# Inverse roots of the norms: a power on GpSimd in place of a square root on ScalarE and a reciprocal on VectorE

## The chip, the cores and the metric

The kernel runs on one core of one Trainium2 chip. The metric is the device time of one execution in microseconds (us); lower is better. One core has five engines with instruction queues of their own: TensorE (PE in the profile; PEld is its weight load), VectorE (DVE), ScalarE (ACT), GpSimd (POOL) and SyncE (SP), which here only issues DMAs. Each queue runs in its own order and waits by semaphores for what other engines produce.

## The reference

The network has 16 stages in a row on an x of 4 batches x 512 tokens x 128 features, float32. Each stage is an attention, a feed-forward or a state-space block on a layer norm of x, added to x:

```python
def _layernorm(x, axis=-1, eps=1e-05):
    m = jnp.mean(x, axis=axis, keepdims=True)
    v = jnp.var(x, axis=axis, keepdims=True)
    return (x - m) / jnp.sqrt(v + eps)

x = x + _L0_attn_a_ref(_layernorm(x, axis=-1), ...)
x = x + _L0_ffn_ref(_layernorm(x, axis=-1), ...)
...
x = x + _L3_ffn_ref(_layernorm(x, axis=-1), ...)
```

Two stages have inverse roots of their own. L1a scales each token of its output by `lax.rsqrt(mean(square(y)) + 1e-6)`. L1b norms its input a second time, `x * lax.rsqrt(mean(x * x) + EPS) * w`, and its output as well, with EPS = 1.1920929e-07.

## The kernel before

x stays in SBUF as 16 tiles of 128 tokens x 128 features, four to a batch; batches are called b0 to b3. The stages run in the order L0a, L0f, L0b, L0f, L1a, L1f, L1b, L1f, L2a, L2f, L2b, L2f, L3a, L3f, L3b, L3f: "a" and "b" are the two mixers of a layer, "f" its feed-forward block.

The layer norm is spread over three engines. When a batch of x has been updated (x<-x,ps in line 443, one VectorE instruction of 128x512), `moments` takes mean and variance of its four tiles on VectorE (bn_stats, bn_aggr: ln_st and ln_mv in the profile). `roots` then turns the variances of one to three batches into inverse roots (ln_rs): one square root on ScalarE with eps as its bias (line 385), and one reciprocal on VectorE (line 389). A root of three batches has 12 columns, that of one batch 4. `centred` writes xn = (x - mean) * root, one VectorE instruction for each of the four tiles of a batch (line 393). `transposed` turns xn on TensorE into PSUM (ps_tr, line 351) and copies it on ScalarE to xT (line 365), from which the stage's matmuls (all in line 346) read. After xn of a batch, GpSimd adds the output bias to x in some stages (x<-x,rows, line 438).

Near the end of a stage the norm of b0 to b2 is made for the next one (`normed_ahead`), while b3 is still computed; b3's own root, four columns, follows at the start of the next stage or within it.

A table of ScalarE functions must be active before its functions run. Square root, exp, silu, sigmoid and tanh need several, and the compiler puts a load (ACT_TABLE_LOAD, booked on the line of the instruction that needs it) wherever the next function isn't in the active one. `prime` (line 410) is an activation on one column whose only effect is to have the table loaded at that place.

The order of each engine's queue is made by a scheduler when the program is built, from its own estimates, except that instructions given to `keep_in_program_order` keep the order of the source among each other on their engine. The square root in `roots` is given to it always; the reciprocal and the centring only where the caller passes `keep`. TensorE's matmuls are nearly all given to it.

In L1a, `output` takes the mean of squares of a batch on TensorE (ps_m), the root of it in line 1353 and 1368 (rs, 4 columns), and adds the product to x (line 1371). In L1b, `roots` (lines 1500 to 1505) takes two roots of the same variances, one with 1 + EPS and EPS * 1e-5 folded in, side by side in a tile rs of 2 x 16 columns, and `finish` takes 8 columns (two batches) through `rsqrt` (line 355). What else comes up below: the memsets of L0b's v (line 809) and nm (816), L0f's sm_m and sm_e (softmax of the router, 472 to 474) and sg (740), L2b's and L3b's wc (2014), da (2343) and hc (2362, 2367), L1a's mask and th (1152, 1120), and L3f's rz (2627, at the end of L3a) and h (2790).

Of the kernel before, what the change touches and what calls it, by code (L numbers as in the profile page):

```python
# [11 lines left out]
F32 = mybir.dt.float32  # L12
AF = mybir.ActivationFunctionType
ALU = mybir.AluOpType
# [4 lines left out]
P = 128  # L19
B, S, D = 4, 512, 128  # L20
# [12 lines left out]
class Pack:  # L33
# [3 lines left out]
    def __init__(self):  # L37
        self.groups = {}
        self.at = {}
        self.rows = {"rows": [], "late": []}  # L40
        self.row_at = {}
# [233 lines left out]
class Net:  # L275
    def __init__(self, ctx, tc, pk, dram):
        self.ctx, self.tc, self.nc, self.pk = ctx, tc, tc.nc, pk
        nc = self.nc
        cp = ctx.enter_context(tc.tile_pool(name="const", bufs=1))
        self.cp = cp  # L280
        self.x = cp.tile([P, NC, D], F32, name="x")

        self.st = cp.tile([P, NC, 6], F32, name="ln_st")
        self.mv = cp.tile([P, NC, 2], F32, name="ln_mv")
        self.rs = cp.tile([P, NC], F32, name="ln_rs")
        self.xn = cp.tile([P, NC, D], F32, name="xn")
        self.xT = cp.tile([P, NT], F32, name="xT")
        self.final = self.ahead = False
        self.extra = ()

        x_in = dram["x"].rearrange("b (j p) d -> p (b j) d", p=P)
        for b in range(B):
            nc.sync.dma_start(self.x[:, CB * b : CB * b + CB], x_in[:, CB * b : CB * b + CB])
        self.w, self.dram = {}, dram
        self.second, self.first, self.zeroth = ExitStack(), ExitStack(), ExitStack()
        self.l1a, self.m0 = ExitStack(), ExitStack()
        second = self.second.enter_context(tc.tile_pool(name="second", bufs=1, side="right"))
        first = self.first.enter_context(tc.tile_pool(name="first", bufs=1, side="right"))
        zeroth = self.zeroth.enter_context(tc.tile_pool(name="zeroth", bufs=1, side="right"))
        self.load(cp, "const")  # L300
        self.load(zeroth, *FIRST[:1])
        self.rows = {}
        self.load_rows(cp, "rows")
        self.load(first, *FIRST[1:])
        self.load(second, *SECOND)

        self.ident = cp.tile([P, P], F32, name="ident")
        make_identity(nc, self.ident)
        self.ones = cp.tile([P, P], F32, name="ones")
        nc.gpsimd.memset(self.ones, 1.0)  # L310
        self.eps = {}
        for n, v in (("1e-5", 1e-5), ("1e-6", 1e-6), ("f32", 1.1920929e-07)):
            self.eps[n] = cp.tile([P, 1], F32, name="eps" + n.replace("-", "_"))
            nc.gpsimd.memset(self.eps[n], v)
        self.primed = cp.tile([P, 1], F32, name="primed")

    def load(self, pool, *groups):
# [34 lines left out]
        if pin:  # L352
            self.tc.keep_in_program_order(i)

    def rsqrt(self, out, in_, eps, scale=1.0):

        self.nc.scalar.activation(out, in_, AF.Sqrt, bias=self.eps[eps], scale=scale)
        self.nc.vector.reciprocal(out, out)

    def transposed(self, pp, tag, outT, tok, pin=False):  # L360

# [20 lines left out]

    def roots(self, b0, b1, keep=lambda i: i):
        cs = slice(CB * b0, CB * b1)
        i = self.nc.scalar.activation(
            self.rs[:, cs], self.mv[:, cs, 1], AF.Sqrt, bias=self.eps["1e-5"]
        )
        self.tc.keep_in_program_order(i)
        keep(self.nc.vector.reciprocal(self.rs[:, cs], self.rs[:, cs]))

    def centred(self, b, keep=lambda i: i):
        for c in range(CB * b, CB * b + CB):
# [14 lines left out]

    def prime(self, fn):

        i = self.nc.scalar.activation(self.primed, self.eps["1e-5"], fn)  # L410
        self.tc.keep_in_program_order(i)

    def norm(self, pp, first=B - 1):
# [761 lines left out]
    def L1a(self):  # L1175
# [3 lines left out]
        nc, tc = self.nc, self.tc  # L1179
        with ExitStack() as es:  # L1180
# [3 lines left out]
            keep = tc.keep_in_program_order  # L1184
# [154 lines left out]
            def output(b):  # L1339
                pm = pp.tile([P, CB], F32, tag="mm", name="ps_m")  # L1340
                for j in range(CB):
                    for g in range(2):
                        self.mm(
                            pm[:, j : j + 1],
                            sq[b][:, g, j * P : j * P + P],
                            self.ones[:, 0:1],
                            start=g == 0,
                            stop=g == 1,
                            pin=True,
                        )  # L1350
                rs = rp.tile([P, CB], F32, name="rs")
                keep(
                    nc.scalar.activation(
                        rs, pm, AF.Sqrt, bias=self.eps["1e-6"], scale=1.0 / D
                    )
                )
                px = pp.tile([P, CB, D], F32, tag="mm", name="ps_x")
                for j in range(CB):
                    for g in range(2):
                        self.mm(  # L1360
                            px[:, j],
                            gt[b][:, g, j * P : j * P + P],
                            self.W("a1_ow")[:, g * P : g * P + P],
                            start=g == 0,
                            stop=g == 1,
                            pin=True,
                        )
                nc.vector.reciprocal(rs, rs)
                xb = self.x[:, CB * b : CB * b + CB]
                for j in range(CB):  # L1370
                    nc.vector.scalar_tensor_tensor(
                        xb[:, j], px[:, j], rs[:, j : j + 1], xb[:, j], ALU.mult, ALU.add
                    )
                self.moments(b)
# [11 lines left out]
            for b in range(B):  # L1386
                self.bias_x(b, "a1_ob")
                keys(b)
                within(b, 0)
                if b + 1 < B:  # L1390
                    features(b + 1, "k", 0)
                else:
                    self.prime(AF.Sqrt)
                    output(0)
                products(b)
                others(b)
                if b == 0:
                    self.normed(B - 1, B)
                    self.prime(AF.Silu)
                if b + 1 < B:  # L1400
                    features(b + 1, "k", 1)
                else:
                    output(1)
                within(b, 1)
                if b + 1 < B:
                    for g in range(2):
                        features(b + 1, "q", g)
                    values(b + 1)
                    gate(b + 1)
                else:  # L1410
                    output(2)
                if b == 0:
                    turned(B - 1)
                if b < 2:
                    self.ternary(f"w{b + 1}", pp.tile([P, 1], F32, tag="mm", name="ps_w"))
                sums(b)
# [58 lines left out]
    def L1b(self):  # L1475
# [4 lines left out]
        nc, tc = self.nc, self.tc  # L1480
        SC, EPS, LAG = 32.0**-0.5, 1.1920929e-07, 3
        with (
# [9 lines left out]

            mv = self.mv
            rs = sp.tile([P, 2, NC], F32, name="rs")
            tiny = sp.tile([P, 1], F32, name="tiny")
            nc.gpsimd.memset(tiny, EPS * 1e-5)
            x0 = sp.tile([P, NC, D], F32, name="x0")
            xh, xT = self.xn, self.xT

            def roots(b0, b1):  # L1500
                cs = slice(CB * b0, CB * b1)
                var = mv[:, cs, 1]
                nc.scalar.activation(rs[:, 0, cs], var, AF.Sqrt, bias=tiny, scale=1.0 + EPS)
                nc.scalar.activation(rs[:, 1, cs], var, AF.Sqrt, bias=self.eps["1e-5"])
                nc.vector.reciprocal(rs[:, :, cs], rs[:, :, cs])


            def centred(out, b, k, eng):
# [31 lines left out]
            q, k, v, ema, a, aT, cT, mixed, y, t = ({} for _ in range(10))  # L1540
# [98 lines left out]
            def finish(b0):  # L1639

                m2 = ms[:, CB * b0 : CB * b0 + 2 * CB]
                self.rsqrt(m2, m2, "f32", scale=1.0 / D)
                for b in (b0, b0 + 1):
                    for j in range(CB):
                        c = CB * b + j
# [807 lines left out]
    def L3a(self):  # L2453
# [3 lines left out]
        nc, tc = self.nc, self.tc  # L2457
        H = S // 2
        with ExitStack() as es:
            sp = es.enter_context(tc.tile_pool(name="l3a_s", bufs=1))  # L2460
            pp = es.enter_context(tc.tile_pool(name="l3a_p", bufs=2, space=PSUM))
            keep = tc.keep_in_program_order
# [4 lines left out]
                out=tri,  # L2467
                in_=tri,
# [42 lines left out]
            bias = self.W("a3_b")  # L2511
            one = self.ones[:, 0:1].to_broadcast([P, S])
            f, ex, v, km, em, wt, kc, r, rz, pv, po, ps = ({} for _ in range(12))
# [166 lines left out]
            for b in range(B):  # L2680
# [35 lines left out]
                masked(b, 3)  # L2716
                if b == 0:
                    self.normed(B - 1, B)
                    self.prime(AF.Exp)
                if b + 1 < B:  # L2720
                    values(b + 1)
                    for i in range(4):
# [21 lines left out]
    def L3f(self):  # L2744

        nc, tc = self.nc, self.tc
        keep = tc.keep_in_program_order
        with (
# [61 lines left out]
            self.mamba_turn(2, bank)  # L2810
            inputs(1)
            self.normed(B - 1, B)
            self.prime(AF.Sigmoid)
            states(1)
            inputs(2)
            self.mamba_turn(3, bank)
# [103 lines left out]
```

## Time and profile before

| | |
|---|---|
| median of 3 runs | 2416.75 us (2408.03 to 2416.97) |
| the profiled execution | 2416.53 us, its span 2414.5 us |
| granted TensorE clock, mean | 0.931 of full |
| square roots on ScalarE in line 385 | 31, about 0.30 us each |
| reciprocals in line 389 | 31, 0.17 to 0.23 us |
| table loads on ScalarE, all lines | 109, 1.283 us each |
| centring on VectorE, line 393 | 240, median 0.342 us |

A row of the profile's timeline reads: start in us, length in us, engine, line, operation, the tile written and the tiles read, partitions x elements, and how many alike were joined. In square brackets stands how long the engine had been idle before it, and what it waited for. The answer for one line lists its instructions with the shortest, median and longest duration in ns, and then who sat waiting for them, how long and how many times.

### The profile page before, as it was taken

The numbers are of one execution on the slowest core, as the hardware profiler recorded it, in microseconds if no ns is written. First come the engines' busy times: TensorE is split into PE (matmuls) and PEld (weight loads), VectorE is DVE, ScalarE is ACT, GpSimd is POOL, SyncE is SP. The second block draws the span as 40 slices with busy tenths as digits, with TensorE's granted clock in tenths as the row PEclk, the third lists the DMA queues.
The fourth block names the chain that finished last, engine by engine and source line by source line (L and its number), as shares of the span: only waits on it lengthen the run. The fifth ranks groups of instructions, "written<-read, shape, count | busy, mean of one in ns | idle before, by whom it ended". The sixth has DMA issues, their size and how long they took to land.

```text
span 2414.5 us, 33686 instructions
## 1 busy us (share of the span) xinstructions
PE 2154.8 (89%) x12151; PEld 1017.6 (42%) x12151; DVE 1731.8 (72%) x3413; ACT 1287.0 (53%) x2550; POOL 610.7 (25%) x443
## 2 busy tenths in 40 slices
PE   7999999999899998999877789888869998888868
PEld 2343334643333334667444446542214666422213
DVE  6666666589998775656464674678997657678995
ACT  4555555279845665342442453666655445466643
POOL 1100010010000001022162410038872014248871
PEclk9999999999899998998866989998989999998989
DMA  3000001400000000410200025334542520044540
GB/s 144 1 1 1 1 1 43 100 1 2 2 1 2 1 1 18 109 18 13 97 1 1 0 46 91 67 122 139 159 146 51 95 49 2 1 121 141 161 152 18
DMA packets 68886, 127.85 MB, mean 53 GB/s; under 512 B 9329, under 2 KB 29297, under 8 KB 68081
## 3 DMA queue, kind: packets, MB, share of 16 engines
q1 hardware_dynamic: 68720, 125.71, 19.6%
q8 instruction: 96, 1.57, 0.3%
q14 instruction: 70, 0.57, 0.1%
HBM read 119.91 MB, written 5.64 MB: 52 GB/s over the span
## 4 chain that ended last, share of the span: by engine, by line
PE 65%; DVE 16%; issue 8%; ACT 6%; DMA 2%; POOL 1%; SPq 1%; POOLq 0%; DVEq 0%; ACTq 0%
PE ps_o L346 14%; PE ps_s L346 9%; PE ps_st L346 6%; PE ps_c L346 5%; PE ps L346 4%; PE ps_g L346 4%; DVE hc L2362 3%; PE ps_x L346 3%; PE ps_u L346 2%; PE ps_v L346 2%; PE ps_qk L346 2%; PE ps_du L346 2%; DVE ps_du L2357 2%; PE ps_tr L351 2%; DVE e L839 2%
## 5 line engine op out<-in xcount | busy, mean ns | idle before, releaser
L2367 POOL TENSOR_TENSOR hc<-hc,cr 128x1024 f32<-128x1024 f32 x126 | 297.4, 2361 | 113.8 <-DVE hc L2362 107.9
L2362 DVE TENSOR_TENSOR_SCAN hc<-da,ps_du 128x1024 f32<-128x1024 f32 x128 | 291.1, 2276 | 0.0
L346 PE MATMUL ps_s<-k,q 32*128 32x512 f32 (+3 forms) x1088 | 256.6, 601 | 10.8 <-DVE mx L839 8.6
L538 ACT ACTIVATE e<-ps_s,mx 128x512 f32<-128x512 f32 x256 | 172.6, 686 | 139.4 <-DVE mx L533 132.8
L346 PE MATMUL ps_du<-du,spread 64*128 64x512 f32 x512 | 162.1, 705 | 66.0 <-DVE hc L2362 65.7
L2343 ACT ACTIVATE da<-da,am 128x512 f32<-128x512 f32 x248 | 166.3, 716 | 63.7 <-DMA da<-dram 48.8
L346 PE MATMUL ps<-xT,w_L2f 128*128 128x512 f32 (+1 forms) x416 | 193.1, 611 | 0.0
L925 DVE TENSOR_REDUCE nm<-ps_s 128x1 f32<-128x512 f32 x256 | 162.7, 684 | 37.5 <-PE ps_s L346 27.8
L1011 ACT ACTIVATE e<-ps_st 128x512 f32<-128x512 f32 x256 | 138.4, 595 | 88.7 <-PE ps_s L346 61.1
L533 DVE TENSOR_REDUCE mx<-ps_s 128x2 f32<-128x1024 f32 x128 | 150.9, 1219 | 43.8 <-PE ps_s L346 43.6
L2357 DVE TENSOR_TENSOR ps_du<-ps_du,br 128x1024 f32<-128x1024 f32 x128 | 155.0, 1211 | 26.9 <-PE ps_du L346 26.9
L850 ACT ACTIVATE e<-e,mx 128x512 f32<-128x512 f32 (+3 forms) x256 | 140.3, 550 | 21.9 <-DVE mx L839 21.3
L346 PE MATMUL ps_st<-q,k 32*128 32x512 f32 x512 | 143.7, 645 | 0.0
L346 PE MATMUL ps_s<-q,k 64*128 64x512 f32 x512 | 129.1, 618 | 2.2 <-ACT e L538 1.7
L346 PE MATMUL ps_c<-e,vz 128*64 128x512 f32 x512 | 123.5, 604 | 0.8 <-POOL vz L549 0.8
L1934 DVE SCALAR_TENSOR_TENSOR t<-ps,w_L2f,t 128x512 f32<-128x512 f32 (+1 forms) x104 | 76.7, 747 | 61.6 <-PE ps L346 39.7
L346 PEld LDWEIGHTS ps_s<-k,q 32*128 32x128 f32 x1088 | 89.0, 192 | 75.0 <-DVE mx L839 50.2
L346 PEld LDWEIGHTS ps_du<-du,spread 64*128 64x128 f32 x512 | 45.9, 203 | 175.0 <-issue 115.0
L839 DVE CUSTOM_DVE_ANT_0 e<-ps_s,tri 128x512 f32<-128x512 f32 (+3 forms) x256 | 109.6, 485 | 8.8 <-PE ps_s L346 8.8
L346 PEld LDWEIGHTS ps<-xT,w_L2f 128*128 128x128 f32 (+1 forms) x416 | 75.5, 190 | 95.8 <-issue 75.5
L549 POOL TENSOR_TENSOR vz<-v,z 128x512 f32<-128x512 f32 x32 | 33.4, 1044 | 321.9 <-DVE z L547 292.9
L659 DVE TENSOR_TENSOR hc<-hc,wt 128x1024 f32<-128x1024 f32 x80 | 94.7, 1188 | 23.1 <-ACT hc L1937 12.2
(499 smaller groups left out, 4199.8 us busy)
## 6 DMA issues: line engine op xcount, KB each, us to landing
da<-dram SPq DMA_DIRECT2D x124, 256.0 KB
da<-dram SPq DMA_DIRECT2D x124, 255.5 KB
wt<-dram SPq DMA_DIRECT2D x144, 128.0 KB
wt<-dram SPq DMA_DIRECT2D x32, 256.0 KB
dram<-dl SPq DMA_DIRECT2D x16, 256.0 KB
wt<-dram SPq DMA_DIRECT2D x16, 224.0 KB
wt<-dram SPq DMA_DIRECT2D x16, 192.0 KB
wt<-dram SPq DMA_DIRECT2D x16, 160.0 KB
```

The source lines that it names most:

```text
L346: i = self.nc.tensor.matmul(out, lhsT, rhs, start=start, stop=stop)
L533: nc.vector.tensor_reduce(mx, sc, AX.X, ALU.max, negate=True)
L538: nc.scalar.activation(es[n][:, hh], sc[:, hh], AF.Exp, bias=mx[:, hh : hh + 1], accum_out=z[m][:, j, hh : hh + 1],)
L659: nc.vector.tensor_tensor(h, h, wt[b, k][:, r:e], ALU.mult)
L839: red = nc.vector.tensor_tensor_reduce(e[:, i, :w], sc[i][:, :w], tri[:, S - w :], -1.0, BIG, ALU.add, ALU.min, mx[:, i : i + 1],)
L850: nc.scalar.activation(e[:, i, :w], e[:, i, :w], AF.Exp, bias=mx[:, i : i + 1], scale=-1.0, accum_out=z[:, i : i + 1],)
L925: nc.vector.tensor_reduce(nm[:, j, i, 9:10], sc, AX.X, ALU.max, negate=True)
L1011: keep(nc.scalar.activation(es_[n][:, i], sc, AF.Exp))
L2343: nc.scalar.activation(da[n][:, t, t:], src[:, t:], AF.Exp, scale=am[:, at : at + 1])
L2357: keep(nc.vector.tensor_tensor(dx[n], dx[n], br, ALU.mult))
L2362: keep(nc.vector.tensor_tensor_scan(h, a, x, 0.0, ALU.mult, ALU.add))
L2367: keep(nc.gpsimd.tensor_tensor(hc[n], hc[n], cr, ALU.mult))
```

## The change

The inverse root is no longer a square root on ScalarE and a reciprocal on VectorE. `roots` adds eps to the variance on GpSimd and raises the sum there to the power -0.5, against a column of -0.5 broadcast over the operand. `rsqrt`, and the roots of L1b, do the scaling and the adding on VectorE and the power on GpSimd. None of these instructions is pinned unless the caller passes `keep`; the square root was. Four primes go: those for the square root and back to silu in L1a, that for exp in L3a after b0, and the second for sigmoid in L3f. Of the columns of constants, the three eps and L1b's tiny go, `some` and `half` come.

```diff
-    def rsqrt(self, out, in_, eps, scale=1.0):
-        self.nc.scalar.activation(out, in_, AF.Sqrt, bias=self.eps[eps], scale=scale)
-        self.nc.vector.reciprocal(out, out)
+    def rsqrt(self, out, in_, eps, scale, keep=lambda i: i):
+        keep(self.nc.vector.tensor_scalar(out, in_, scale, eps, ALU.mult, ALU.add))
+        self.inverse(out, keep)
+
+    def inverse(self, a, keep=lambda i: i):
+        half = self.half.to_broadcast(list(a.shape))
+        keep(self.nc.gpsimd.tensor_tensor(a, a, half, ALU.pow))
...
     def roots(self, b0, b1, keep=lambda i: i):
         cs = slice(CB * b0, CB * b1)
-        i = self.nc.scalar.activation(
-            self.rs[:, cs], self.mv[:, cs, 1], AF.Sqrt, bias=self.eps["1e-5"]
-        )
-        self.tc.keep_in_program_order(i)
-        keep(self.nc.vector.reciprocal(self.rs[:, cs], self.rs[:, cs]))
+        keep(self.nc.gpsimd.tensor_scalar(self.rs[:, cs], self.mv[:, cs, 1], 1e-5, None, ALU.add))
+        self.inverse(self.rs[:, cs], keep)
...
                 rs = rp.tile([P, CB], F32, name="rs")
-                keep(
-                    nc.scalar.activation(
-                        rs, pm, AF.Sqrt, bias=self.eps["1e-6"], scale=1.0 / D
-                    )
-                )
+                self.rsqrt(rs, pm, 1e-6, 1.0 / D)
...
-                nc.vector.reciprocal(rs, rs)
                 xb = self.x[:, CB * b : CB * b + CB]
...
                 else:
-                    self.prime(AF.Sqrt)
                     output(0)
                 products(b)
                 others(b)
                 if b == 0:
                     self.normed(B - 1, B)
-                    self.prime(AF.Silu)
...
             def roots(b0, b1):
                 cs = slice(CB * b0, CB * b1)
                 var = mv[:, cs, 1]
-                nc.scalar.activation(rs[:, 0, cs], var, AF.Sqrt, bias=tiny, scale=1.0 + EPS)
-                nc.scalar.activation(rs[:, 1, cs], var, AF.Sqrt, bias=self.eps["1e-5"])
-                nc.vector.reciprocal(rs[:, :, cs], rs[:, :, cs])
+                nc.vector.tensor_scalar(
+                    rs[:, 0, cs], var, 1.0 + EPS, EPS * 1e-5, ALU.mult, ALU.add
+                )
+                nc.vector.tensor_scalar(rs[:, 1, cs], var, 1e-5, None, ALU.add)
+                self.inverse(rs[:, :, cs])
...
-                self.rsqrt(m2, m2, "f32", scale=1.0 / D)
+                self.rsqrt(m2, m2, EPS, 1.0 / D)
...
                 if b == 0:
                     self.normed(B - 1, B)
-                    self.prime(AF.Exp)
...
             self.normed(B - 1, B)
-            self.prime(AF.Sigmoid)
             states(1)
```

More of the change, by code (lines that the diff above doesn't have):

```diff
@@ L310, in __init__ @@
         nc.gpsimd.memset(self.ones, 1.0)
[L311 to L314, printed above, removed]
+        self.some = cp.tile([P, 1], F32, name="some")
+        nc.gpsimd.memset(self.some, 1e-5)
+        self.half = cp.tile([P, 1], F32, name="half")
+        nc.gpsimd.memset(self.half, -0.5)
         self.primed = cp.tile([P, 1], F32, name="primed")
@@ L408, in prime @@
     def prime(self, fn):
-        i = self.nc.scalar.activation(self.primed, self.eps["1e-5"], fn)
+        i = self.nc.scalar.activation(self.primed, self.some, fn)
         self.tc.keep_in_program_order(i)
@@ L1494, in L1b @@
             rs = sp.tile([P, 2, NC], F32, name="rs")
-            tiny = sp.tile([P, 1], F32, name="tiny")
-            nc.gpsimd.memset(tiny, EPS * 1e-5)
             x0 = sp.tile([P, NC, D], F32, name="x0")
```

## The prediction, made before the changed kernel ran

> **What bounds the kernel now.** I read the page first: busy time by engine, then the chain that ended last.
>
> ```profile
> PE 2154.8 (89%) x12151; PEld 1017.6 (42%) x12151; DVE 1731.8 (72%) x3413; ACT 1287.0 (53%) x2550; POOL 610.7 (25%) x443
> PE 65%; DVE 16%; issue 8%; ACT 6%; DMA 2%; POOL 1%; SPq 1%; POOLq 0%; DVEq 0%; ACTq 0%
> ```
>
> TensorE sets the end, but a third of the chain lies elsewhere, at the seams between stages, where TensorE waits for a normed x. The answer for the line that takes the square root shows what the change can touch.
>
> ```profile
> L385 ACT ACTIVATE ln_rs<-ln_mv,eps1e x31: 296/300/319, 8.9 to 2386.7; 128x4 f32<-128x4 f32 x16, 128x12 f32<-128x12 f32 x14, 128x8 f32<-128x8 f32 x1
> L385 ACT ACT_TABLE_LOAD  x20: 1283/1283/1283, 7.6 to 2385.4; - x20
>   DVE ln_rs L389: 19.5, 18
>   PEld ps_tr L351: 5.9, 2
> ```
>
> 20 of the 31 roots load a table first, at 1.283 us, and VectorE stood idle for 19.5 us in 18 waits for a root. But the root costs more than that: it is pinned in ScalarE's queue, so all that follows from it comes late. The timeline at the start of L2a shows it best.
>
> ```profile
> 1345.43 0.69 DVE L443 TENSOR_TENSOR x<-x,ps_o 128x512 f32<-128x512 f32 x1 [4.77 <-PE ps_o L346]
> 1346.91 1.28 ACT L385 ACT_TABLE_LOAD   x1
> 1348.21 0.30 ACT L385 ACTIVATE ln_rs<-ln_mv,eps1e 128x12 f32<-128x12 f32 x1
> 1348.98 0.23 DVE L389 RECIPROCAL ln_rs<-ln_rs 128x12 f32<-128x12 f32 x1
> 1349.24 5.06 DVE L393 TENSOR_SCALAR xn<-x,ln_mv,ln_rs 128x128 f32<-128x128 f32 x12
> 1349.73 1.41 PE L351 MATMUL ps_tr<-ident,xn 128*128 128x128 f32 x5 [4.41 <-DVE xn L393]
> 1354.63 3.06 PE L346 MATMUL ps_d<-xT,wd 128*128 128x512 f32 x4
> ```
>
> Three of the four batches had their variance before 1345, while VectorE sat idle for 4.77 us; their root ran at 1348.21, TensorE was idle for 4.41 us and reached its first matmul at 1354.63.
>
> **The change, part by part.** *Removed from ScalarE:* the compiled order has 79 table loads in place of 109 (30 x 1.283 = 38.5 us, net of one more switch in each L0f), 39 square roots of 0.30 us and 4 primes of 0.20 us; in all about 51 us of 1287. That is busy time on an engine that holds 6% of the chain, so nearly all is hidden under TensorE. *Removed from VectorE:* 39 reciprocals (0.18 to 0.29 us, about 7.5 us), against 10 small scalings added at the 0.2 us of such rows. Hidden the same way.
>
> *Added to GpSimd:* 31 adds and 37 powers. No row shows a power. The bounds come from the nearest rows:
>
> ```profile
> L2010 POOL TENSOR_SCALAR am<-am x2: 290/292/293, 1425.2 to 2120.4; 128x32 f32<-128x32 f32 x2
> L1796 POOL TENSOR_TENSOR wd<-w_L2a x2: 451/453/455, 1345.5 to 1345.9; 128x128 f32<-128x128 f32 x2
> ```
>
> From below, a power of 12 columns is no dearer than an ordinary operation: 0.25 us. From above, it costs what 1024 columns cost in two-input work, 2.36 us (hc<-hc,cr), some 85 times as much an element. I take 0.8 us for 12 columns, 0.5 for 4 and 1.2 for 24: nearer the low end, because the columns are so few, and about thrice the 0.29 us of am. With an add of 0.25 us and the hops between engines the root is then ready about 1.2 us after the variance; the old one took 2.3 us with a load (1346.91 to xn at 1349.24) and 0.6 without (499.49 to 500.05).
>
> The Trainium skill speaks against the placement: "GPSIMD Engine Reference", section 4.1 Engine selection, sends elementwise work to VectorE and calls GpSimd some two times slower with two inputs. By twice VectorE's 0.18 us a power would cost an estimated 0.4 us, which would take about 4 us off the sum below; no run here shows a power.
>
> *Moved:* the scheduler, no longer held by the pinned ScalarE instruction, sets the centring (xn) earlier in VectorE's order. The opposite cost is that a root now stands in GpSimd's queue, behind memsets and behind x+rows (1.27 us each), and xn, placed early in VectorE's in-order queue, holds whatever follows it. TensorE's order is the same in both. I went through each seam of the trace, with that order beside it; bounds in brackets:
>
> - Start: batch 3's root ran at 13.68 behind three copies on ScalarE, its xn at 14.23; now xn follows the others at 12.6: -1.3 (-1.6 to +0.5).
> - L0b to L0f, 929: xn of three batches waited for a root at 928.91; now it runs among the reductions of 885 on. TensorE's waits there (2.58 + 1.21 us before transposes, first ps_l at 937.07, could start near 933): -4.2 (-5 to -2). Behind xn of batch 3 now stands the softmax's sm_e; its power follows two th (1.56 each) and the mask on GpSimd and ends near 935.9, still 3 us ahead of the old time.
> - L1a, 1065.9: load, root, load, prime take ScalarE 3.0 us between two qk activations, ps_qk being ready at 1067.8: -1.5 (-2.9 to 0).
> - L1a's end, 1144: transposes waited 3.94 us for x, which stood behind xn x12: -2.2 (-4 to 0).
> - L1f to L2a, as shown: 12 xn done by the last x, ps_d at about 1348.5: -5.5 (-7 to -3).
> - L2a to L2f, 1400: root and load before; eight of 12 xn now come before the clash shown below: -2.5 (-4 to +1).
> - L2f, 1469.8 and 1561.0: load and root between two activations, transposes idle 1.63 and 2.10 us: -3.5 together (-5 to -1).
> - L2b's start, 1589.4: a prime's load in front of the first da: -1.0 (-1.4 to 0).
> - L3a, 2002.3: load, root, load, prime; transposes idle for 3.96 us: -2.7 (-3.9 to 0).
> - L3f, 2102.3: the load back (1.28) delays the second h: -1.7 (-2 to 0).
>
> These sum to -26.1 us. Against them stand the places where GpSimd is late:
>
> ```profile
> 498.30 1.81 POOL L809 MEMSET v<- 128x2048 f32 x1
> 499.49 0.32 ACT L385 ACTIVATE ln_rs<-ln_mv,eps1e 128x4 f32<-128x4 f32 x1
> 500.05 1.38 DVE L393 TENSOR_SCALAR xn<-x,ln_mv,ln_rs 128x128 f32<-128x128 f32 x4
> 501.36 0.73 DVE L775 TENSOR_SCALAR q<-ps_qk,w_const 128x512 f32<-128x512 f32 x1
> ...
> 1402.35 2.34 POOL L2014 TENSOR_TENSOR wc<-w_L2b,late 128x1024 f32<-128x1024 f32 x1
> 1402.37 2.54 DVE L393 TENSOR_SCALAR xn<-x,ln_mv,ln_rs 128x128 f32<-128x128 f32 x1
> ```
>
> - L0b's start: the power queues behind the v memset and an nm memset (0.53), to start near 500.9; xn at 501.5 and q behind it: +1.5 (+0.5 to +3).
> - L1b's start: before, three batches' roots were done by 1178.8 and xn ran at 1180.11; the compiled order has both scalings and the 24-column power after the last x: +1.7 (+0.8 to +4).
> - L3f's start: one xn now stands ahead of the 1.75 us reciprocal of rz, and waits for the power until 2063.2: +0.9 (+0.3 to +2.5).
> - L0f's two extra switches, 1.28 us each, mostly under TensorE: +1.0 (0 to +2.6).
>
> These sum to +5.1. The last two lines of the fence show a further risk: a 0.34 us xn took 2.54 us beside a GpSimd operation of 2.34. Powers are short, so I price this at nothing; if they held VectorE, 37 x 0.5 = 18 us at most. The other seams (L0a's end, L1a's start, L2b's end, L3b's start and end, L3f's gates at 2081 and 2385) I put at nothing: there TensorE is busy without a gap, or waits for ps_o, while the root runs.
>
> Net: -26.1 + 5.1 = -21.0, from the profiled execution's 2416.5 us (span 2414.5 and 2.0 around it, within 0.3 us of the median): **2395.5 us**. Adding all the best ends gives -35, all the worst +8.
>
> "ScalarE: Activation LUTs", section What ACT_TABLE_LOAD costs, adds a drain of 1.38 us to the load, 2.66 us a switch. Here the root's ACTIVATE follows the load within 20 ns (1346.91 + 1.28, then 1348.21); by the page 30 loads would be 80 us of ScalarE, by the row 38.5.
>
> **Rivals.** *Hidden anyway (0.16):* for it speaks that only 5.9 us of TensorE's waits are put down to the root itself, and that ScalarE is idle for half the span. Then -5.9 and +5.1 cancel: about 2416. Against it, waits on xn count too (28.5 us of PE ps_tr in 11 waits).
>
> *Slower, the power is dear (0.12):* with VectorE's queue in order, some ten places have something urgent behind an early xn or x (start, L0b, L1a's output, L1b's start and its two outputs, L2a, L3a, and L3f's two roots). Each us that a power takes above 0.8 costs some 10 us there; the gain is gone at 2.9 us, and at 5 us the sum is -21 + 42 = +21: 2437. It decides from about 4 us. Against it, 2.36 us is the longest ordinary GpSimd row; for it, that no trace here has a power.
>
> *Larger gain (0.12):* all the best ends, 2381, if the power is as cheap as an add.
>
> **How the numbers follow.** Forecast 0.60. A measurement tells about 0.5% from no change: 12.1 us, so faster is below 2404.7 and slower above 2428.8. Of the forecast's 0.60, 0.57 lies below 2404.7; with the larger gain 0.69 faster; 0.16 + 0.03 the same; 0.12 slower. Range 2381 (all best ends) to 2416 (hidden anyway); the likeliest case's own is 2384 to 2406.
>
> **What would show it.** 79 table loads and ScalarE near 1236 us busy; the power's row near 0.5 to 0.8 us; ps_d at L2a's start some 6 us sooner after the last ps_o; no wait of transposes near 929 and 2004; xn later than before at L0b's and L1b's starts. Wrong if the power's row is over 2.5 us, if VectorE's waits for ln_rs grow beyond the 19.5 us of now, or if TensorE's gaps at the seams merely get another releaser.

## The result, and the profile after

| | before | after |
|---|---|---|
| median | 2416.75 us (2408.03 to 2417.15, 5 runs) | 2436.84 us (2429.19 to 2438.86, 5 runs) |
| profiled execution, its span | 2416.53, 2414.5 us | 2430.64, 2428.9 us |
| table loads on ScalarE | 109 | 79 |
| ScalarE busy, GpSimd busy | 1287.0, 610.7 us | 1236.1, 684.3 us |

The changed kernel takes 1.0095 of the time of the kernel before (95% interval 1.0078 to 1.0111): 0.95% slower, where 0.9% faster was forecast. What was to be removed is gone (30 loads, 51 us of ScalarE, as worked out), and GpSimd has 74 us more. The page of after, busy time by engine and the chain that ended last:

```profile
PE 2156.3 (89%) x12151; PEld 1021.5 (42%) x12151; DVE 1721.3 (71%) x3384; ACT 1236.1 (51%) x2474; POOL 684.3 (28%) x511
PE 64%; DVE 16%; issue 8%; ACT 5%; POOL 3%; DMA 2%; SPq 1%; DVEq 0%; ACTq 0%; POOLq 0%
```

ScalarE gave one percent of the chain away and GpSimd took two. The groups of GpSimd's line 363, the power, kept apart by shape (busy us, mean ns), and then two rows of after's waits (us in total, times, longest):

```profile
L363 POOL TENSOR_TENSOR ln_rs<-ln_rs,half 128x12 f32<-128x12 f32 x14 | 32.2, 2297 | 1.1
L363 POOL TENSOR_TENSOR ln_rs<-ln_rs,half 128x4 f32<-128x4 f32 x16 | 16.6, 1038 | 1.1
L363 POOL TENSOR_TENSOR rs<-rs,half 128x24 f32<-128x24 f32 x1 | 4.2, 4166 | 30.3 <-DVE ln_mv L380 30.3
L363 POOL TENSOR_TENSOR ms<-ms,half 128x8 f32<-128x8 f32 x2 | 3.3, 1668 | 9.7 <-DVE ms L357 9.7
```
```profile
DVE xn L395 <- POOL ln_rs L363: 42.9, 23, 3.3
PE ps_tr L351 <- DVE xn L395: 17.0, 4, 11.4
```

A power takes 1.04, 1.67, 2.30 and 4.17 us at 4, 8, 12 and 24 columns: a straight line, 0.41 us and 0.156 us a column. VectorE waits 42.9 us for it, where it waited 19.5 us for the square root. Three places show what that does. The end of L0a in after's timeline:

```profile
346.35 2.29 POOL L363 TENSOR_TENSOR ln_rs<-ln_rs,half 128x12 f32<-128x12 f32 x1
348.68 0.86 DVE L395 TENSOR_SCALAR xn<-x,ln_mv,ln_rs 128x128 f32<-128x128 f32 x3 [2.75 <-POOL ln_rs L363]
349.45 1.22 DVE L535 TENSOR_REDUCE mx<-ps_s 128x2 f32<-128x1024 f32 x1
350.76 0.69 ACT L540 ACTIVATE e<-ps_s,mx 128x512 f32<-128x512 f32 x1 [6.26 <-DVE mx L535]
```

The xn of the next stage stands in VectorE's queue ahead of mx, which L0a's softmax is waiting for, some 40 us before the next stage's transposes. VectorE stands still for 2.75 us, and ScalarE's next e waits for mx. The start of L2a:

```profile
1355.47 2.30 POOL L363 TENSOR_TENSOR ln_rs<-ln_rs,half 128x12 f32<-128x12 f32 x1
...
1357.81 5.05 DVE L395 TENSOR_SCALAR xn<-x,ln_mv,ln_rs 128x128 f32<-128x128 f32 x12 [2.83 <-POOL ln_rs L363]
1362.78 0.67 DVE L445 TENSOR_TENSOR x<-x,ps_o 128x512 f32<-128x512 f32 x1
1365.75 2.56 PE L346 MATMUL ps_d<-xT,wd 128*128 128x512 f32 x3
```

The 12 xn do run ahead of the last x, as foretold, but begin 2.8 us late and hold that x until 1362.78, though the last ps_o ended at 1359.3 (1355.73 and 3.55). ps_d starts 3.0 us after x; before it was 9.2 (1345.43 to 1354.63), but x itself came at once there. And L0b's start:

```profile
502.54 1.81 POOL L811 MEMSET v<- 128x2048 f32 x1
504.31 0.24 POOL L390 TENSOR_SCALAR ln_rs<-ln_mv 128x4 f32<-128x4 f32 x1
504.98 1.05 POOL L363 TENSOR_TENSOR ln_rs<-ln_rs,half 128x4 f32<-128x4 f32 x1
506.06 1.34 DVE L395 TENSOR_SCALAR xn<-x,ln_mv,ln_rs 128x128 f32<-128x128 f32 x4 [3.33 <-POOL ln_rs L363]
507.32 0.74 DVE L777 TENSOR_SCALAR q<-ps_qk,w_const 128x512 f32<-128x512 f32 x1
```

The power stands behind the two memsets as the prediction had it; q follows xn.

TensorE's 12151 matmuls have the same order in both kernels, but for three pairs of neighbours, so a matmul's start after, less its start before (the offset), gives the loss place by place. The growth of that offset across each place of the prediction, in us, and the same for the run e1_mult told below:

| place | predicted | after | e1_mult |
|---|---|---|---|
| start | -1.3 | -1.3 | -3.0 |
| L0a's end | 0 | +3.3 | +1.2 |
| L0b's start | +1.5 | +4.3 | +1.0 |
| L0b's end, into L0f | -4.2 | +0.4 | -7.4 |
| L0f (two more switches) | +1.0 | -2.3 | -1.4 |
| L1a's start | 0 | +2.7 | +0.7 |
| L1a, root of b3 | -1.5 | -2.0 | -2.0 |
| L1a's own roots and end | -2.2 | +2.3 | -2.9 |
| L1b's start | +1.7 | +5.4 | +5.2 |
| L1b's outputs | 0 | +3.6 | +1.7 |
| L1f to L2a | -5.5 | -3.0 | -6.0 |
| L2a to L2f | -2.5 | +1.1 | -1.5 |
| L2f, two roots | -3.5 | -2.8 | -2.7 |
| L2b's start | -1.0 | -0.5 | -0.5 |
| L3a | -2.7 | +2.0 | -4.6 |
| L3f's start | +0.9 | +2.1 | 0.0 |
| L3f, second h | -1.7 | +0.9 | 0.0 |
| the rest | 0 | -1.8 | -1.4 |
| sum | -21.0 | +14.4 | -23.6 |

Two rows hold a loss and a gain that nearly cancel. At L0b's end the early xn waits for its power in the middle of L0b's reductions (VectorE stands still for 2.76 us before 892.40), and after loses 5.7 us there (e1_mult 2.5, e2_twice 8.2); at the seam itself it then gains 5.4 (e1_mult 10.6). In the L3a row after loses 7.8 us from the end of L2f on (1971 to 2000 of before; e1_mult 1.4), and then gains 6.1 at batch 3's root, as e1_mult does. So the gains at these seams came even with the long power; the losses lie ahead of them.

### The profile page after: what moved, and what is told of

Read it like the earlier page. It is cut to its first block, busy times and chain, and to the rows that moved or that the text cites. A ratio compares the mean times of both kernels' runs of the same rounds, so it can differ in the third digit from the quotient of the medians.

```text
span 2428.9 us, 33627 instructions
## 1 busy us (share of the span) xinstructions
PE 2156.3 (89%) x12151; PEld 1021.5 (42%) x12151; DVE 1721.3 (71%) x3384; ACT 1236.1 (51%) x2474; POOL 684.3 (28%) x511
## 4 chain that ended last, share of the span: by engine, by line
PE 64%; DVE 16%; issue 8%; ACT 5%; POOL 3%; DMA 2%; SPq 1%; DVEq 0%; ACTq 0%; POOLq 0%
PE ps_o L346 13%; PE ps_s L346 9%; PE ps_st L346 6%; PE ps L346 5%; PE ps_c L346 4%; PE ps_g L346 4%; DVE hc L2357 3%; PE ps_x L346 3%; PE ps_u L346 2%; DMA wt<-dram 2%; DVE e L841 2%; PE ps_qk L346 2%; PE ps_v L346 2%; PE ps_du L346 2%; PE ps_tr L351 2%
## 5 line engine op out<-in xcount | busy, mean ns | idle before, releaser
L2338 ACT ACTIVATE da<-da,am 128x512 f32<-128x512 f32 x248 | 165.9, 715 | 63.7 <-DMA da<-dram 51.3
L390 POOL TENSOR_SCALAR ln_rs<-ln_mv 128x4 f32<-128x4 f32 (+2 forms) x31 | 9.9, 318 | 559.0 <-DVE ln_mv L380 555.8
```

The source lines that it names most:

```text
L2338: nc.scalar.activation(da[n][:, t, t:], src[:, t:], AF.Exp, scale=am[:, at : at + 1])
```

## The experiments

All ratios are to the kernel before, run on the same chip beside each; intervals are 95%. The bands in us that were expected for the first four runs were made beside before's 2416.75; in these runs before took 2407.74, so the ratios are the fairer measure. "Theory A" is that the power's length is what costs, "theory B" that its place is.

| run | median us | before, us | ratio |
|---|---|---|---|
| e1_mult | 2392.66 | 2407.74 | 0.9935 (0.9909 to 0.9961) |
| e2_twice | 2479.49 | 2407.74 | 1.0301 (1.0275 to 1.0328) |
| e3_own_back | 2418.47 | 2407.74 | 1.0043 (1.0024 to 1.0062) |
| e4_split | 2417.19 | 2407.74 | 1.0035 (1.0019 to 1.0052) |
| e5_best | 2393.62 | 2410.84 | 0.9925 (0.9905 to 0.9945) |
| e6_late | 2438.74 | 2410.84 | 1.0108 (1.0083 to 1.0133) |
| e7_late_mult | 2425.96 | 2410.57 | 1.0070 (1.0054 to 1.0085) |
| e8_best2 | 2387.19 | 2410.57 | 0.9913 (0.9897 to 0.9930) |

### e1_mult: the power's length taken away

```diff
-        nc.gpsimd.memset(self.half, -0.5)
+        nc.gpsimd.memset(self.half, 1.0)
...
-        keep(self.nc.gpsimd.tensor_tensor(a, a, half, ALU.pow))
+        keep(self.nc.gpsimd.tensor_tensor(a, a, half, ALU.mult))
...
-        keep(self.nc.gpsimd.tensor_scalar(self.rs[:, cs], self.mv[:, cs, 1], 1e-5, None, ALU.add))
+        keep(self.nc.gpsimd.tensor_scalar(self.rs[:, cs], self.mv[:, cs, 1], 0.0, 0.05, ALU.mult, ALU.add))
```

`rsqrt` and L1b's roots get the same constant.

> The changed kernel with a multiplication by 1.0 in place of each power, on the same tiles, and the column before it set to a constant 0.05 by the same instruction: every queue holds the same instructions in the same order, only the power's duration is gone. It leaves out the inverse root itself (every norm multiplies by 0.05). Theory A (the power is dear: its rows took 1.04, 1.67, 2.30 and 4.17 us at 4, 8, 12 and 24 columns, and VectorE, in order, stood 42.9 us in 23 waits for it): 2395 to 2405 us, VectorE's waits for ln_rs under 15 us. Theory B (the place is what costs: the root behind memsets and x+rows in GpSimd's queue, xn too early in VectorE's): 2425 to 2437 us, as the changed kernel.

The ratio is 0.9935: faster than before. In us it lies just under the band that A gave; as a ratio to 2416.75 it would be 2401, inside it. Two of its groups of line 363, and its wait:

```profile
L363 POOL TENSOR_TENSOR ln_rs<-ln_rs,half 128x4 f32<-128x4 f32 x16 | 3.8, 241 | 1.1
L363 POOL TENSOR_TENSOR ln_rs<-ln_rs,half 128x12 f32<-128x12 f32 x14 | 2.9, 210 | 1.2
```
```profile
DVE xn L395 <- POOL ln_rs L363: 14.3, 16, 2.7
```

With 0.21 us in place of 2.30 for 12 columns, and nothing else moved in any queue, the whole loss is gone. B falls: the place alone costs nothing net. Nor does the power slow VectorE's own work beside it, the risk that the prediction put at nothing: 17 us of VectorE's instructions run at the same time as a power in after, and they take 0.1 us more in all than the same instructions in e1_mult.

### e2_twice: the length doubled

```diff
         half = self.half.to_broadcast(list(a.shape))
+        one = self.ones[:, :1].to_broadcast(list(a.shape))
         keep(self.nc.gpsimd.tensor_tensor(a, a, half, ALU.pow))
+        keep(self.nc.gpsimd.tensor_tensor(a, a, one, ALU.pow))
```

> The changed kernel with a second power, exponent 1.0, behind each power: the result is the same, each root takes another 1.0 to 4.2 us. Theory A: the loss grows as it came, by some 6 to 10 us for each us that a root is longer, so 2448 to 2462 us, VectorE's waits for ln_rs about 80 us. Theory B: GpSimd's queue gets 37 more short instructions, 2435 to 2442 us.

Ratio 1.0301, more than A asked for. The second power, and VectorE's wait:

```profile
L365 POOL TENSOR_TENSOR ln_rs<-ln_rs,ones 128x12 f32<-128x12 f32 x14 | 31.7, 2266 | 1.0
L365 POOL TENSOR_TENSOR ln_rs<-ln_rs,ones 128x4 f32<-128x4 f32 x16 | 16.3, 1016 | 1.0
```
```profile
DVE xn L397 <- POOL ln_rs L365: 89.8, 25, 5.8
```

With e1_mult and the changed kernel this makes three points. Line 363 is busy for 8.5 us in e1_mult and 63.7 in after, a step of 55; the second powers here add 64. The profiled executions take 2392.6, 2430.6 and 2479.4 us: 38 us for 55 and 49 for 64, so 0.69 and 0.76 us of the end for each us of power. The scheduler also moved some instructions on VectorE, ScalarE and GpSimd here; in e1_mult every queue has after's order.

### e3_own_back: only the layer norms changed

`rsqrt`, L1a's rs and L1b's roots, with the prime for the square root in L1a, are put back as in the kernel before; `roots` stays on GpSimd.

```diff
-                self.rsqrt(rs, pm, 1e-6, 1.0 / D)
+                keep(
+                    nc.scalar.activation(
+                        rs, pm, AF.Sqrt, bias=self.eps["1e-6"], scale=1.0 / D
+                    )
+                )
...
-                self.inverse(rs[:, :, cs])
+                nc.scalar.activation(rs[:, 0, cs], var, AF.Sqrt, bias=tiny, scale=1.0 + EPS)
+                nc.scalar.activation(rs[:, 1, cs], var, AF.Sqrt, bias=self.eps["1e-5"])
+                nc.vector.reciprocal(rs[:, :, cs], rs[:, :, cs])
```

> The changed kernel, but L1a's and L1b's own roots (rs, ms) as they were before: square root on ScalarE, reciprocal on VectorE. The 31 roots of the layer norms stay powers on GpSimd. Theory A, by how TensorE's offset between the two traces grew around those eight roots (+1.5 in L1a, +5.5 at L1b's start, +3.2 at L1b's outputs): about 10 us less than the changed kernel, 2423 to 2430 us. Theory B puts nothing on their length, and the layer norms' roots are as before: 2432 to 2440 us.

1.0043, against 1.0095 for the whole change: the eight roots of L1a and L1b cost about 0.5%, or 12 us. The median lies under the band; on 2416.75 the ratio would give 2427, inside it. The offset stays within 0.5 us through L1b (after: +9.0).

### e4_split: a root for each batch

```diff
-        self.roots(b0, b1, keep)
+        for b in range(b0, b1):
+            self.roots(b, b + 1, keep)
         for b in range(b0, b1):
             self.centred(b, keep)
```

> The changed kernel with a root for each batch (add and power of 4 columns) in place of one of 12 columns for three batches. The powers of the first two batches can run long before the third's variance is there, and the last takes 1.04 us and not 2.30. Theory A: the stalls of VectorE fall to about half of 42.9 us, 2420 to 2430 us. Theory B: more instructions in GpSimd's queue and xn no later in VectorE's, 2434 to 2445 us.

The ratio is 1.0035, which on 2416.75 would be 2425, in A's band. But VectorE's wait, in the same view as above, did not halve; it grew:

```profile
DVE xn L396 <- POOL ln_rs L363: 52.5, 37, 3.3
```

So the sum of that wait does not rank the versions. By the offset, L0a as a whole and L0b's end gained (from +3.3 to +2.2 and from +0.4 to -7.4 us), but 10.7, 7.0 and 10.8 us were lost in L2b, L3a and L3b. There a root that waits for its variance stands in GpSimd's queue in front of hc and em; that it blocks them is read from the order, and was not tried alone. In e5_best below, where these three norms have one root of 12 columns again, at most 1.7 us is lost in each of the three.

### e6_late: the centring set behind the running stage

```diff
+        late = self.tc.keep_in_program_order if b1 - b0 == B - 1 else keep
         for b in range(b0, b1):
-            self.centred(b, keep)
+            self.centred(b, late)
```

> The changed kernel with the centring of three batches (xn after a root of 12 columns) kept in program order, which sets it behind the reductions of the stage that is still running; the powers stay where they are. Theory A in its narrow form (the loss is VectorE standing still in its own order for a root, with the reductions of the running stage behind it): VectorE waits for ln_rs under 25 us, ratio to before 0.997 to 1.005. Theory C (TensorE waits for xn itself, so a long root costs wherever xn stands): waits as before the edit or worse, ratio 1.008 to 1.015.

Both halves of the narrow form cannot stand together: the wait fell as it asked, and the time did not. Ratio 1.0108. Two rows of its waits, and then the second row's counterpart in the kernel before:

```profile
PE ps_tr L351 <- DVE xn L396: 52.0, 16, 12.0
...
DVE xn L396 <- POOL ln_rs L363: 11.0, 8, 2.6
```
```profile
PE ps_tr L351 <- DVE xn L393: 28.5, 11, 10.0
```

VectorE waits little now (11.0 us for 42.9), and TensorE waits more: 17.0 us in the changed kernel, 52.0 here. Centred late, the 12 xn lie on the seam; centred early, they hold VectorE for the power.

### e7_late_mult: late and short

e6_late with e1_mult's edit.

> e6_late with e1_mult's multiplication in place of the power (same queues in the same order; it leaves out the inverse root, every norm multiplies by 0.05). It parts the gain of e1_mult (ratio 0.9935) into its two sources. If the gain comes from centring early (xn done before the seam between stages), it is gone here although the power is short and the table loads are gone: ratio 0.998 to 1.004. If it comes from the 30 table loads and 39 square roots that ScalarE no longer does, it stays: 0.990 to 0.996.

1.0070, above both bands. The same 30 loads and 39 square roots are gone as in e1_mult, and yet it is slower than before, so e1_mult's net gain needs the early centring. That the loads bring nothing doesn't follow: kept in program order, the xn come later than in the kernel before, and TensorE waits 47.8 us for them, where it waited 28.5.

By the offset the work taken off ScalarE does bring something. At four places the same matmuls gain the same in every version, whatever the power's length and wherever the xn stand: 2.0 us at batch 3's root in L1a, 3.95 and 2.3 to 2.7 at L2f's two roots, and 6.1 at batch 3's root in L3a; in e7_late_mult 14.7 us together. The last of them in the kernel before:

```profile
2002.30 1.28 ACT L385 ACT_TABLE_LOAD   x1
2003.60 0.30 ACT L385 ACTIVATE ln_rs<-ln_mv,eps1e 128x4 f32<-128x4 f32 x1
2003.91 1.28 ACT L410 ACT_TABLE_LOAD   x1
...
2004.93 1.16 PE L351 MATMUL ps_tr<-ident,xn 128*128 128x128 f32 x4 [3.96 <-DVE xn L393]
```

How much of this is the loads and how much the pinned place of the root wasn't parted. Power against multiplication is worth 0.4% when xn is late (1.0108 to 1.0070) and 1.6% when it is early (1.0095 to 0.9935).

### e5_best and e8_best2: what follows from these

e5_best: e4_split's edit except in three norms (those made for the feed-forward after L2b, after L3a and after L3b), and L1b's roots on ScalarE as before. The first lines:

```diff
+        self.calls = getattr(self, "calls", 0) + (b1 - b0 == B - 1)
+        one = b1 - b0 == B - 1 and self.calls not in (10, 12, 13)
+        for b in range(b0, b1, 1 if one else b1 - b0):
+            self.roots(b, b + 1 if one else b1, keep)
```

> What the runs so far recommend put together: a root for each batch as in e4_split, but not at the three places where TensorE's offset grew by 7 to 11 us there (the norms made ahead for the feed-forward after L2b, after L3a and after L3b, which keep the root of 12 columns), and L1b's own roots on ScalarE as in e3_own_back. L1a's stay powers. Theory A, adding the offsets by stage (about -24 us by L2b, -8 for L1b, nothing lost after): 0.983 to 0.992 of the kernel before, 2372 to 2393 us where before takes 2410. Theory B: no better than e4_split, 1.000 to 1.004.

0.9925 (0.9905 to 0.9945): just above A's band, clear of B's. In e8_best2 the first L3f's roots go back to ScalarE as well:

```diff
+        if getattr(self, "calls", 0) == 12:
+            i = self.nc.scalar.activation(
+                self.rs[:, cs], self.mv[:, cs, 1], AF.Sqrt, bias=self.some
+            )
+            self.tc.keep_in_program_order(i)
+            keep(self.nc.vector.reciprocal(self.rs[:, cs], self.rs[:, cs]))
+            return
```

> e5_best with the roots of the first L3f (after L3a, four of them) back on ScalarE and VectorE, pinned and primed as before the change. There TensorE's offset grew by 4.7 us in e5_best. Theory A: 3 to 5 us less than e5_best, ratio 0.990 to 0.9915. If the square roots' table loads cost as much there as the powers: 0.992 to 0.994.

0.9913 (0.9897 to 0.9930), in A's band: 2387.19 us against 2410.57. By the times it can't be told from e5_best, as the intervals overlap. By the offset it can at the place itself: from L3f's start on, through its last root, the offset falls by 2.9 us where it rose by 4.4 in e5_best. This version beats the kernel before by 0.9% and the changed one by 1.8%.

## Why the prediction was wrong

The step that failed is the price of the power with the slope put on it, "I take 0.8 us for 12 columns, 0.5 for 4 and 1.2 for 24" and "Each us that a power takes above 0.8 costs some 10 us". The power took 2.30 us for 12 columns, and its length is worth 38 us of the end between e1_mult and after, the whole loss and more.

*The size.* 2.30, 1.04 and 4.17 us were measured: the upper bound of 2.36, not the lower, for 12 columns, and beyond it for 24, which a bound without a slope by columns could not hold. The reason given, that the columns are so few, held for the multiplication (0.21 us) and not for the power.

*The slope.* With the measured 2.30 us that rule gives -21 + 10 x 1.5 = -6 us, still no loss. e1_mult, after and e2_twice give 0.69 to 0.76 us of the end for each us of power. The kernel has 39 powers and not 37 (31 for the layer norms, 8 for L1a and L1b), so one us more on each is 39 us, and some 27 to 30 us of the end, not 10. The prediction counted ten places with something urgent behind an early xn. At L0a's end and L1a's start it put nothing, "TensorE is busy without a gap", and at L0b's end it counted the seam's gain and nothing for the reductions among which the xn now stand. By the table, after less e1_mult, the 38 us lie mostly at L0b's end (7.8), in L3a (6.6), at L1a's own roots and end (5.2), at L0b's start (3.3), into L2a (3.0) and L2f (2.6); L0a's end and L1a's start, with 2.1 and 2.0, are the smaller part.

*What held.* 51 us went off ScalarE, and by far not all of it came off the time, as said; at the four places told under e7_late_mult the gain is 14.7 us where the forecast had 7.7. The map of places is right in sign where the root is short: L0b's end (-7.4 for -4.2), L1a's b3 (-2.0 for -1.5), L2a (-6.0 for -5.5), L2f (-2.7 for -3.5) and L3a (-4.6 for -2.7). With the power's real length the same places gave +0.4, -2.0, -3.0, -2.8 and +2.0. That e1_mult's offsets sum to -23.6, near the forecast's -21.0, is partly luck: its root is shorter than the 0.8 us of the forecast, and beside before's median e1_mult gains only 15 us. L0f's two switches cost nothing that shows (-2.3 for +1.0). L3f's second h gained nothing (0.0 for -1.7). L0b's start was named as a loss with its cause, and under-priced (+4.3 for +1.5); L1b's start likewise (+5.4 for +1.7), though there e1_mult, with its short root, loses nearly as much (the last section).

*The rivals.* The one that came true is "the power is dear". Its mechanism was right; its point of decision was put at 4 us of a power, and 2.30 sufficed. "Hidden anyway" would have given the old time. "Larger gain", 2381, would not have come with the multiplication's price either: e1_mult's ratio makes 2401 of 2416.75. The weight of 0.12 rested on "2.36 us is the longest ordinary GpSimd row", which says nothing of an operation that has no row.

*The sign to look for.* "VectorE's waits for ln_rs grow beyond the 19.5 us" did come true (42.9), but it is no measure: e4_split has 52.5 and is faster than the changed kernel, e6_late 11.0 and is no faster. The other sign, a power of over 2.5 us, did not come at 12 columns, and the loss did.

*The base.* The sum was made against a profiled execution at the top of the runs of before; beside the experiments, before takes 2407.7 to 2410.8. That is worth up to 9 us of the forecast, and none of its sign.

## What to carry to other kernels

An operation without a row in the trace is priced by a run or by its worst bound, and a slope by its elements belongs to the bound; when a change hangs on it, measure that first. Take the pinned instruction out of a chain and the scheduler sets all that follows from it earlier: on an engine that works in order this is a gain only while the new producer is short, so ask for each such place what stands behind the early consumer. Here a root made per batch on GpSimd, except in the three norms where that lost, and left on ScalarE in L1b and in the first L3f, is worth 0.9%.

## What the runs showed of the hardware that was not expected

On 128 partitions GpSimd's power costs 0.41 us and 0.156 us a column, at 12 columns some 11 times its multiplication (2.30 against 0.21 us). The two exponents tried, -0.5 and 1.0, take nearly the same (2.297 and 2.266 us). The Trainium skill, "GPSIMD Engine Reference", section 4.1 Engine selection, sends elementwise work to VectorE and calls GpSimd some two times slower for two inputs. The slower time here goes the way of that advice; its factor isn't tested, because no run has a power on VectorE. Against the 0.23 us of VectorE's reciprocal of 12 columns in the kernel before, the power is ten times as long.

A short wait can be followed by a slow stretch. At L1b's start e1_mult's first transposes were only 0.5 us later against the last ps_o than before (TensorE idle for 2.91 us where it was 2.38), yet the offset grew by 5.2 us. Windows of before, and then of e1_mult, from the same matmul on (us, then busy us of PE, PEld, DVE, ACT, POOL with the number of instructions, granted clock, DMA share, GB/s):

```profile
1185.00:1200.00 15.00, 10.83 (x45) 4.48 (x44) 8.39 (x16) 9.02 (x21) 5.54 (x4) 0.96 0.00 1
```
```profile
1170.00:1185.00 15.00, 14.20 (x37) 5.92 (x36) 5.87 (x10) 8.55 (x20) 2.57 (x2) 0.56 0.01 2
```

The granted clock is 0.96 in the one and 0.56 in the other, and fewer matmuls keep TensorE busy for longer. The 45 matmuls of the first line take e1_mult 19.35 us, 16.36 of them busy, at 0.65. In the trace's clock records the stretch at half clock that begins ahead of these matmuls lasts 3.41 us in before and 17.07 us in e1_mult.

Over the whole span the clock was 0.938 in e1_mult, 0.930 in after, 0.923 in e2_twice and 0.941 in e8_best2. It doesn't simply follow the time or TensorE's idle time: e4_split, as slow as before and with more idle time (282 against 260 us), has 0.939 where before has 0.931. The skill's "TensorE: Matmul & The Clock Gate", Part 1, has the clock at half after an idle window of about 3.4 us; neither gap here is that long, so the page doesn't tell the two apart. Of the 38 us between e1_mult and after, 15.3 are longer busy time of the same matmuls (2141.0 and 2156.3 us) and the rest is idle time. Which gap sets off which slow stretch stays open.
